# Layer 1 of the last two batches from edge lists for six of eight node tiles

## The chip, the cores and the metric

The kernel runs on one core of a Trainium2 chip. The time is the device time of one execution in microseconds (us), and the figure is the median over several runs. A profiled execution has its own time and a span from its first to its last instruction. In the profile, PE is TensorE, PEld its weight loads, DVE VectorE, ACT ScalarE, POOL GpSimd and SP SyncE, which here only issues DMAs.

## The reference, cut to what matters

Sixteen batches of 1024 nodes with 256 features go through four graph layers. All share one weighted adjacency matrix of 1024 x 1024, in which about 1.6% of the entries (some 17 of a row) are not zero.

```python
x, adj: (16, 1024, 256), (1024, 1024)      # float32
# layer 0: scores only matter where A is not zero
S   = sigmoid(relu(pre_u[:, :, None] + pre_v[:, None] + b1) @ W2 + b2)
a_t = einsum('buv,bud->bvd', S * A, h);  m_t = einsum('uv,bud->bvd', A, h) * h
x   = beta1 * h + beta2 * (a_t @ Wa + ba) + beta3 * (m_t @ Wm + bm)
# layer 1: the layer that is changed
msg = einsum('ij,bjd->bid', A, x)
msg = einsum('bid,ed->bie', msg, W) + b
x   = x + relu(msg)
# layers 2 and 3: attention with a bias
feats = x @ W1.T;  f1 = feats @ W2 + b2
coefs = softmax(leaky_relu(f1[:, :, None] + f1[:, None, :]) + A, axis=-1)
x     = coefs @ feats + bias2 + x
```

## The kernel before

**Groups and pairs.** Batches are taken in four groups of four. For every group, `with_edges` multiplies the scored adjacency with the features (layer 0's edge part), and then `pair_layers` takes the group's batches two by two through layers 1, 2 and 3. The state of a batch is `z`, features on partitions, 2 x 1024 per partition.

**Layer 1 by matmul.** `pair_layers` first projects: `y = z W`, nodes on partitions, 32 matmuls for the two batches, each bank evacuated by ScalarE (L1102). Then, for each half of the nodes, SP loads eight 128x512 blocks of the transposed adjacency from DRAM (`adjT_in`, L1111, three buffers), and TensorE multiplies each with both batches' `y`. ScalarE adds the bias and applies ReLU (L1122), VectorE adds the result to `z` (L1123).

**Layers 2 and 3.** `front` computes features (`feats`, `g_wT`), and `sums` has VectorE build the weights `m` tile by tile (L1033) for TensorE to multiply with `feats`. `finish` scales the result, transposes (L1141, L1165) and adds it.

**Lists.** At the start the kernel finds each node's neighbours: `slot_v` holds up to 32 neighbour numbers of each node and `slot_a` their weights. The first 16 are used directly. Of the rest, in fours, only those groups that are not empty are packed into `XT` = 6 extra tiles of 128 rows (`x_node`, `x_a`); `to_u` says in which row of these each group lies. The lists serve layer 0's scores: GpSimd gathers rows of `v_d` by `slot_v` with an indirect DMA (`fetch`, `gather`, L692), VectorE and ScalarE compute the score (L802, L804, L808), and GpSimd scatters it into `dense_d` (L697).

**Order.** Main work is a generator that yields its estimated TensorE time in us; `Side.along` runs `rate` steps of the side work for each such microsecond. `RATE[1]` is 0.255 beside groups. `paced` makes an instruction wait for the matmul six before the latest one written, so that it does not run ahead of TensorE. Matmuls are recorded by `product` (L125). Instructions on one engine execute in the order of a compile-time schedule, which may differ from the order in which they are written. The side work of a group (its scores) has to be finished before the group's `with_edges`; beside the fourth group there is none left.

```python
for g in range(NGR):
    hw, z = loaded.pop(0)
    while g not in finished:
        next(side.steps)
    side.along(with_edges(g, hw, z), RATE[1])
    side.along(pair_layers(g * GB, z[:2], lambda: None), RATE[1])
    side.along(pair_layers(g * GB + 2, z[2:], lambda: ahead(g + 1)), RATE[1])
```

Of the kernel before, what the change touches and what calls it, by code (L numbers as in the profile page):

```python
# [9 lines left out]
F32 = mybir.dt.float32  # L10
I32 = mybir.dt.int32
U32 = mybir.dt.uint32
AF = mybir.ActivationFunctionType
ALU = mybir.AluOpType
AX = mybir.AxisListType
P = 128

GB = 4
BUFS = 2
RATE = (0.26, 0.255)  # L20
SLOTS = 32
FIRST = 16
EXTRA = SLOTS - FIRST
QUAD = 4
ZERO = 1024
NG = EXTRA // QUAD
XT = 6
HOLD = 40
LEAD = 4
TOP = 16.0  # L30

# [6 lines left out]
def after(tc, ins, others, kind, why):  # L38
    dep = mybir.DependencyInfo(kind, mybir.DependencyReason.DATA)
    for o in others:  # L40
        tc.add_manual_dep(ins.ins, o.ins.name, dep, reason=why)
# [23 lines left out]
def gnn_stack_kernel(  # L65
# [27 lines left out]
    nc = tc.nc  # L93
    B, N, D = x.shape
    NT = N // P
    DH = D // P
    HN = 512
    NV = N // HN
    HT = HN // P
    QN = HN // 2  # L100

    const = ctx.enter_context(tc.tile_pool(name="const", bufs=1))
    dram = ctx.enter_context(tc.tile_pool(name="dram", bufs=1, space=bass.MemoryType.DRAM))
# [3 lines left out]
    def bank():  # L107
        return psum[-1].tile([P, HN], F32, tag="bank", name="bank")
# [8 lines left out]
    def paced(ins, back=6):  # L117


        if recent:  # L120
            after(tc, ins, [recent[max(0, len(recent) - back)]], mybir.DependencyClass.Sync, "keeps pace")
        return ins

    def product(*args, **kw):
        recent.append(nc.tensor.matmul(*args, **kw))  # L125
        del recent[:-BACK]
        return recent[-1]
# [32 lines left out]
    ident = const.tile([P, P], F32, name="ident")  # L160
    make_identity(nc, ident)

    def column(a, name):

        t = const.tile([P, DH], F32, name=name)
        nc.gpsimd.dma_start(t, a.rearrange("(h p) -> p h", p=P))
        return t
# [73 lines left out]
    adjT_d = dram.tile([NT, P, N], F32, name="adjT_d")  # L241
# [3 lines left out]
    NGR = B // GB  # L245
# [9 lines left out]
    TABLE = NG * NT * P  # L255
    WORDS = 16
    extra_d = dram.tile([2 * TABLE, WORDS], F32, name="extra_d")

    slot_v = const.tile([P, NT, SLOTS], U32, name="slot_v")
    slot_a = const.tile([P, NT, SLOTS], F32, name="slot_a")  # L260
# [98 lines left out]
    to_u = const.tile([P, NF], U32, name="to_u")  # L359
    with ExitStack() as stack:  # L360
# [46 lines left out]
        l1b = column(g1_b, "l1b")  # L407
# [44 lines left out]
        ps = bank()  # L452
# [24 lines left out]
        step = 1  # L477
# [10 lines left out]
        to = prep1.tile([P, NF], F32, name="to")  # L488
# [183 lines left out]
    with tc.If(listed > 0) as arm:  # L672
        with ExitStack() as stack:
# [6 lines left out]
            zs = stack.enter_context(tc.tile_pool(name="zs", bufs=2))  # L680
            slot_pool = stack.enter_context(tc.tile_pool(name="slots", bufs=LEAD + 2))
            wide_z = stack.enter_context(tc.tile_pool(name="wide_z", bufs=4))
            wide_t = stack.enter_context(tc.tile_pool(name="wide_t", bufs=5))
            psum_pool(stack, "banks", 8)
            gd_pool = stack.enter_context(tc.tile_pool(name="gd", bufs=4))
# [5 lines left out]
            def gather(dst, src, at, **how):  # L691
                return nc.gpsimd.indirect_dma_start(  # L692
                    out=dst, out_offset=None, in_=src[:], in_offset=bass.IndirectOffsetOnAxis(ap=at, axis=0), **how,
                )
# [6 lines left out]
            def score_steps(pool):  # L701
# [41 lines left out]
                for t in range(NT):  # L743
                    search(own, t)
                    if t == 0:
                        sources(us, *tiles[0])
                        for step in todo[:LEAD]:
                            fetch(us, zt, *step)
# [31 lines left out]
                for n, (g, t, k) in enumerate(todo):  # L780
                    if n + LEAD < len(todo):
                        last = fetch(us, zt, *todo[n + LEAD])
                    for _ in range(0 if n < HOLD else 2 if n % 2 and len(waiting) > 4 else 1):
                        if waiting:
# [53 lines left out]
            def lists(t):  # L838
                if t < NT:
                    return FIRST, slot_v[:, t, :], slot_at[:, t, :], slot_a[:, t, :]  # L840
                return QUAD, x_node[:, t - NT, 1:], x_at[:, t - NT, :], x_a[:, t - NT, :]

            def sources(us, g, t):

                u = us[g, t] = zs.tile([P, GB * D], F32, tag="u", name="u")
                paced(nc.scalar.activation(
                    u.rearrange("p (c k) -> p c k", k=D), b1r[:, None, :].to_broadcast([P, GB, D]), AF.Copy
                ))
                if t < NT:
                    nc.gpsimd.dma_start(u, u_d[g][t * P : (t + 1) * P, :], accum_op=ALU.add)  # L850
                else:
                    gather(u, u_d[g], x_node[:, t - NT, 0:1], compute_op=ALU.add)
# [5 lines left out]
            class Side:  # L858
# [2 lines left out]
                def __init__(self, steps):  # L861
                    self.steps, self.owed = steps, 0.0

                def along(self, main, rate):
                    for us in main:
                        self.owed += us * rate
                        while self.owed >= 1:
                            self.owed -= 1
                            next(self.steps, None)
# [34 lines left out]
            with ExitStack() as first:  # L904
                own1 = first.enter_context(tc.tile_pool(name="own1", bufs=1))
                st_pool = first.enter_context(tc.tile_pool(name="st", bufs=2))
                side = Side(score_steps(own1))
# [49 lines left out]
            three = stack.enter_context(tc.tile_pool(name="three", bufs=3))  # L957
            four = stack.enter_context(tc.tile_pool(name="four", bufs=4))
# [65 lines left out]
            def sums(made, v, finish):  # L1024

                if "f" not in made:
                    catch_up()
                f, r, ta = made["f"], made["r"], made["ta"]
                cols = slice(v * HN, (v + 1) * HN)
                acc = [bank() for _ in range(HT)]  # L1030
                for jt in range(NT):
                    m = four.tile([P, HN], F32, tag="m", name="m")
                    nc.vector.scalar_tensor_tensor(  # L1033
                        m, r[:, cols], ta[:, jt : jt + 1], ea[:, jt, cols], ALU.max, ALU.mult
                    )
                    for c in range(HT):
                        product(
                            acc[c][:, : D + 1], m[:, c * P : (c + 1) * P], f[:, jt, :],
                            start=jt == 0, stop=jt == NT - 1,
                        )  # L1040
                    if jt == 0:
                        catch_up()
                    yield 1.7
                share = small.tile([P, HT], F32, tag="share", name="share")
                for c in range(HT):
                    nc.vector.reciprocal(share[:, c : c + 1], acc[c][:, D : D + 1])
                finish(v, acc, share)
                yield 1.2
# [37 lines left out]
                                ALU.add, ALU.add,  # L1086
                            )

            def pair_layers(b, z, ahead):


                y = [node_major("y") for _ in range(2)]
                for jt in range(0, NT, 2):
                    for i in range(2):
                        ps = bank()
# [7 lines left out]
                            y[i][:, jt : jt + 2, :], ps.rearrange("p (t d) -> p t d", t=2), AF.Copy  # L1103
                        )
                        yield 1.7
                for v in range(NV):
                    cols = slice(v * HN, (v + 1) * HN)
                    acc = [[bank() for _ in range(DH)] for _ in range(2)]
                    for jt in range(NT):
                        a = three.tile([P, HN], F32, tag="a", name="adjT_in")  # L1110
                        nc.sync.dma_start(a, adjT_d[jt][:, cols])  # L1111
                        for i in range(2):
                            for eh in range(DH):
                                product(
                                    acc[i][eh], y[i][:, jt, eh * P : (eh + 1) * P], a,
                                    start=jt == 0, stop=jt == NT - 1,
                                )
                        yield 3.4
                    for i in range(2):
                        for eh in range(DH):  # L1120
                            r = four.tile([P, HN], F32, tag="m", name="r")
                            nc.scalar.activation(r, acc[i][eh], AF.Relu, bias=l1b[:, eh : eh + 1])  # L1122
                            nc.vector.tensor_tensor(z[i][:, eh, cols], z[i][:, eh, cols], r, ALU.add)  # L1123


                def second(i):
# [70 lines left out]
            def ahead(g):  # L1197
                if g < NGR:
                    loaded.append(([load_hw(g * GB + i) for i in range(GB)], load_z(g)))
                    for load, i in z_loads:  # L1200
                        load(i)
                    z_loads.clear()

            for g in range(NGR):
                hw, z = loaded.pop(0)
                while g not in finished:
                    next(side.steps)
                side.along(with_edges(g, hw, z), RATE[1])
                side.along(pair_layers(g * GB, z[:2], lambda: None), RATE[1])
                side.along(pair_layers(g * GB + 2, z[2:], lambda: ahead(g + 1)), RATE[1])  # L1210
            assert next(side.steps, "end") == "end"
            psum.pop()

    with arm.Else():
        with ExitStack() as stack:
# [3 lines left out]
            part = stack.enter_context(tc.tile_pool(name="dpart", bufs=4))  # L1219
# [122 lines left out]
```

## Time and profile before

| | us |
|---|---|
| median of 3 runs | 3267.06 (3267.03 to 3274.82) |
| profiled execution, its own time | 3256.96 |
| its span | 3255.1 |
| TensorE busy | 3157.5 (97%) |
| VectorE busy | 2342.4 (72%) |
| ScalarE busy | 1879.1 (58%) |
| GpSimd busy | 1665.6 (51%) |

The granted clock of TensorE was 0.992 on the mean. Times in the trace are counted from the span's start. A float32 matmul appears as two records. GpSimd's indirect DMAs show as POOL instructions while their descriptors are made; the data arrive later ("landing"). A share of busy time is a mean over very different stages, so the stage around the change has to be read by itself: the fourth group's two pairs, from about 2812 us to the end.

### The profile page before, as it was taken

The page shows a single profiled execution, that of the slowest core. Times are in us where ns is not written, and L with a number is a line of the kernel's source. Part 1 is how long each engine was busy: PE and PEld are TensorE (multiplying, and loading weights), DVE is VectorE, ACT ScalarE, POOL GpSimd, SP SyncE. Part 2 cuts the span into 40 slices and gives each one's busy share as a digit, 9 for nine tenths or more (in the row PEclk, how much of TensorE's full clock was granted, in tenths as well). Part 3 has the DMA queues.
Part 4 walks back from the last instruction along what each step waited for, and adds up shares of the span by engine and source line. Part 5 has one row for each costly group of instructions (what it writes and reads, how often), then busy time and mean ns, then how long its engine had stood idle before and what let it go on. Part 6 is the DMA issues. An engine that isn't in the chain of part 4 may idle for free. (4 is left out here: it accounts for less than half of the span.)

```text
span 3255.1 us, 38756 instructions
## 1 busy us (share of the span) xinstructions
PE 3157.5 (97%) x12162; PEld 2206.3 (68%) x12162; DVE 2342.4 (72%) x3217; ACT 1879.1 (58%) x6316; POOL 1665.6 (51%) x1338
## 2 busy tenths in 40 slices
PE   8899999999997999999999999999999999999999
PEld 5444545545456678578776867778686788778688
DVE  7787767777774799789678979877898881035154
ACT  3245556655667766566886656688666555322132
POOL 1156887686764666657566666665676650000000
PEclk9999999999998999999999999999999999999999
DMA  8998888878798755656875575597656635210100
GB/s 304 327 325 299 281 281 273 273 212 269 242 327 311 219 162 163 203 154 204 292 230 174 154 221 151 183 297 229 180 150 210 186 105 167 84 35 14 55 1 27
DMA packets 268438, 648.91 MB, mean 199 GB/s; under 512 B 42864, under 2 KB 131952, under 8 KB 261056
## 3 DMA queue, kind: packets, MB, share of 16 engines
q0 software_dynamic: 116704, 350.04, 36.8%
q1 hardware_dynamic: 123536, 244.66, 21.8%
q10 hardware_dynamic: 27984, 51.65, 4.2%
q8 instruction: 97, 1.59, 0.2%
q14 instruction: 117, 0.96, 0.1%
HBM read 518.84 MB, written 127.39 MB: 199 GB/s over the span
## 5 line engine op out<-in xcount | busy, mean ns | idle before, releaser
L808 ACT ACTIVATE z<-z 128x256 f32<-128x256 f32 x2432 | 979.7, 406 | 707.3 <-DVE z L804 678.2
L802 DVE TENSOR_TENSOR z<-z,u 128x1024 f32<-128x1024 f32 x608 | 738.8, 1220 | 408.2 <-PE bank L125 276.2
L125 PE MATMUL bank<-feats,m 128*128 128x257 f32 x4096 | 922.1, 383 | 20.8 <-DVE m L1033 18.7
L692 POOL DMA_INDIRECT z<-v_d,slot_v x512 | 645.9, 1262 | 463.8 <-ACT z L808 227.7
L125 PEld LDWEIGHTS bank<-feats,m 128*128 128x128 f32 x4096 | 766.3, 191 | 148.6 <-DVE m L1033 28.6
L804 DVE SCALAR_TENSOR_TENSOR z<-z,w2r 128x1024 f32<-128x1024 f32 x608 | 737.3, 1219 | 8.5
L697 POOL DMA_INDIRECT dense_d<-gt,slot_at x512 | 639.2, 1249 | 197.9 <-issue 134.7
L125 PE MATMUL bank<-gc,hw 128*128 128x256 f32 x2048 | 455.6, 384 | 30.5 <-ACT gc L1061 27.7
L808 ACT ACTIVATION_READ_ACCUMULATOR z<-z 128x1 f32 x2432 | 461.2, 190 | 0.0
L125 PEld LDWEIGHTS bank<-gc,hw 128*128 128x128 f32 x2048 | 387.2, 191 | 98.2 <-ACT gc L1061 40.4
L1033 DVE SCALAR_TENSOR_TENSOR m<-rho,tau,adj_sb 128x512 f32<-128x512 f32 x512 | 374.0, 743 | 107.7 <-PE bank L125 105.1
L125 PE MATMUL bank<-adj_sb,h 128*128 128x512 f32 x1024 | 442.4, 592 | 2.2 <-ACT st L318 2.1
L125 PE MATMUL bank<-adjT_in,y 128*128 128x512 f32 x1024 | 441.3, 592 | 1.4 <-DMA adjT_in<-adjT_d 1.4
L125 PEld LDWEIGHTS bank<-adjT_in,y 128*128 128x128 f32 x1024 | 194.4, 190 | 243.6 <-issue 228.6
L125 PEld LDWEIGHTS bank<-adj_sb,h 128*128 128x128 f32 x1024 | 194.4, 190 | 242.2 <-issue 237.7
L125 PE MATMUL bank<-w,hT 128*128 128x512 f32 (+1 forms) x1024 | 335.8, 488 | 6.8 <-DMA w<-in_L_gnn_W_dram 6.5
L1061 ACT ACTIVATE gc<-gd 128x1024 f32<-128x1024 f32 x128 | 265.5, 2074 | 88.2 <-PE bank L125 60.0
L125 PEld LDWEIGHTS bank<-w,hT 128*128 128x128 f32 x1024 | 195.0, 191 | 150.6 <-issue 126.3
L125 PE MATMUL bank<-g_wT,z 128*128 128x257 f32 x1024 | 232.9, 382 | 0.2 <-ACT st L1171 0.2
L692 POOL DMA_INDIRECT z<-v_d,x_node x96 | 127.1, 1324 | 181.8 <-ACT z L808 118.0
L125 PEld LDWEIGHTS bank<-g_wT,z 128*128 128x128 f32 x1024 | 192.9, 191 | 30.9 <-issue 3.8
L1123 DVE TENSOR_TENSOR z<-z,r 128x512 f32<-128x512 f32 x64 | 42.5, 689 | 135.2 <-ACT r L1122 134.9
(150 smaller groups left out, 2183.4 us busy)
## 6 DMA issues: line engine op xcount, KB each, us to landing
gd<-dense_d SPq DMA_DIRECT2D x128, 512.0 KB, 5.0
dense_d<-zero ACTq DMA_DIRECT2D x64, 512.0 KB, 5.9
adjT_in<-adjT_d SPq DMA_DIRECT2D x128, 256.0 KB, 3.3
h<-in_x_dram SPq DMA_DIRECT2D x19, 1024.0 KB, 12.9
u_d<-st SPq DMA_DIRECT2D x64, 256.0 KB, 5.7
v_d<-st SPq DMA_DIRECT2D x64, 256.0 KB, 6.5
hw_d<-st SPq DMA_DIRECT2D x64, 256.0 KB, 6.5
u<-u_d POOLq DMA_DIRECT2D x32, 512.0 KB, 8.1
```

Of the source, the lines that this page charges most:

```text
L125: recent.append(nc.tensor.matmul(*args, **kw))
L692: return nc.gpsimd.indirect_dma_start(out=dst, out_offset=None, in_=src[:], in_offset=bass.IndirectOffsetOnAxis(ap=at, axis=0), **how,)
L697: return nc.gpsimd.indirect_dma_start(out=dst[:], out_offset=bass.IndirectOffsetOnAxis(ap=at, axis=0), in_=src, in_offset=None,)
L802: paced(nc.vector.tensor_tensor(z, z, u, ALU.add))
L804: nc.vector.scalar_tensor_tensor(zk, zk, 0.0, w2r[:, None, :].to_broadcast([P, GB, D]), ALU.max, ALU.mult)
L808: nc.scalar.activation(zk[:, c, :], zk[:, c, :], AF.Copy, accum_out=s[:, k, c : c + 1])
L1033: nc.vector.scalar_tensor_tensor(m, r[:, cols], ta[:, jt : jt + 1], ea[:, jt, cols], ALU.max, ALU.mult)
L1061: paced(nc.scalar.activation(gc, gd.rearrange("p n i -> p i n"), AF.Copy), 16)
L1123: nc.vector.tensor_tensor(z[i][:, eh, cols], z[i][:, eh, cols], r, ALU.add)
```

## The change

Only the fourth group is treated differently. Its second pair's projection `y` is computed right after `with_edges`, before the first pair (`far_ahead`), and stored to DRAM as `y_d`, one row of 512 numbers (both batches) per node. For node tiles 6 and 7 (`FAR` = 6) the neighbour product stays a matmul with 256 columns of the adjacency. For node tiles 0 to 5, `by_lists` sums it along the first pair's work, 144 steps of one gather and one VectorE instruction:

- 24 steps for the extra tiles, four rows each, into `part`; each finished tile is stored by SP to `part_d`,
- 96 steps for the first 16 neighbours of the nodes of tiles 0 to 5, into `msg`,
- 24 steps that fetch the extra rows' sums from `part_d` and add them to `msg`.

Four gathers are issued ahead of the step that uses them, and `slot_pool` has six buffers. The rate is 0.75 steps per main microsecond for the first 68 (layer 1 of the first pair), then 0.55; what remains then is written in one piece after the first pair. At the head of the second pair `from_lists` transposes `msg` on TensorE, four tiles and then two, and applies bias, ReLU and the add as before (`onto`).

```diff
+FAR = 6
+    y_d = dram.tile([N, 2 * D], F32, name="y_d")
+    part_d = dram.tile([XT * P + P, 2 * D], F32, name="part_d")
...
+            def neighbours(y, z, cols):
+                n = cols.stop - cols.start
+                acc = [[bank() for _ in range(DH)] for _ in range(2)]
+                for jt in range(NT):
+                    a = three.tile([P, HN], F32, tag="a", name="adjT_in")[:, :n]
+                    nc.sync.dma_start(a, adjT_d[jt][:, cols])
+                    for i in range(2):
+                        for eh in range(DH):
+                            product(
+                                acc[i][eh][:, :n], y[i][:, jt, eh * P : (eh + 1) * P], a,
+                                start=jt == 0, stop=jt == NT - 1,
+                            )
+                    yield 3.4 * n / HN
+                onto(z, cols, lambda i, eh: acc[i][eh][:, :n])
...
+            def by_lists(msg):
+                spares = [gd_pool.tile([P, QN, GB], F32, tag="gd", name="msg") for _ in range(4)]
...
+                msg.extend(halves[:FAR])
+                part = halves[FAR:]
+                nc.gpsimd.memset(part[0], 0.0)
+                nc.sync.dma_start(part_d[XT * P :, :], part[0])
+                nc.vector.tensor_scalar(to_u, to_u, float(XT * P), None, ALU.min)
+                todo = [(NT + i, k) for i in range(XT) for k in range(QUAD)]
+                todo += [(t, k) for t in range(FAR) for k in range(FIRST)]
+                todo += [(t, FIRST + q) for t in range(FAR) for q in range(NG)]
...
+                for n, (t, k) in enumerate(todo):
+                    if n + LEAD < len(todo):
+                        fetch_row(*todo[n + LEAD])
+                    z = got.pop((t, k))
+                    to = msg[t] if t < NT else part[t % len(part)]
+                    if t < NT and k >= FIRST:
+                        paced(nc.vector.tensor_tensor(to, to, z, ALU.add))
+                    elif k == 0:
+                        paced(nc.vector.tensor_scalar(to, z, lists(t)[3][:, k : k + 1], None, ALU.mult))
+                    else:
+                        paced(nc.vector.scalar_tensor_tensor(
+                            to, z, lists(t)[3][:, k : k + 1], to, ALU.mult, ALU.add
+                        ))
+                    if t >= NT and k == QUAD - 1:
+                        nc.sync.dma_start(part_d[(t - NT) * P : (t - NT + 1) * P, :], to)
+                    yield
+            def from_lists(z, msg):
+                for t0 in range(0, FAR, HT):
...
+                                nc.tensor.transpose(ps[:, c * P : (c + 1) * P], msg[t][:, at : at + P], ident)
+                    yield 1.2
+                    n = len(tiles) * P
+                    onto(z, slice(t0 * P, t0 * P + n), lambda i, eh: turned_back[i, eh][:, :n])
...
+            def far_ahead(z, main):
+                y = yield from projected(z)
+                both = y_d.rearrange("(t p) (i d) -> p t i d", p=P, i=2)
+                for i in range(2):
+                    nc.sync.dma_start(both[:, :, i, :], y[i])
+                yield from neighbours(y, z, slice(FAR * P, N))
+                gone, far = 0.0, Side(by_lists(msg))
+                def slots():
+                    nonlocal gone
+                    for us in main:
+                        gone += us
+                        yield us * (0.75 if gone < 68 else 0.55)
+                far.along(slots())
+                for _ in far.steps:
+                    pass
+                yield 0
...
-                side.along(pair_layers(g * GB, z[:2], lambda: None), RATE[1])
-                side.along(pair_layers(g * GB + 2, z[2:], lambda: ahead(g + 1)), RATE[1])
+                one = pair_layers(g * GB, z[:2], lambda: None, layer_one(z[:2]))
+                if g < NGR - 1:
+                    side.along(one, RATE[1])
+                    side.along(pair_layers(g * GB + 2, z[2:], lambda: ahead(g + 1), layer_one(z[2:])), RATE[1])
+                else:
+                    for _ in far_ahead(z[2:], one):
+                        pass
+                    for _ in pair_layers(g * GB + 2, z[2:], lambda: None, from_lists(z[2:], msg)):
+                        pass
```

`projected`, `neighbours`, `onto` and `layer_one` hold what stood at the head of `pair_layers`; `layer_one` does what it did there.

## The prediction

> **What bounds the kernel now.** The page first: engine shares, then the slices.
>
> ```profile
> PE 3157.5 (97%) x12162; PEld 2206.3 (68%) x12162; DVE 2342.4 (72%) x3217; ACT 1879.1 (58%) x6316; POOL 1665.6 (51%) x1338
> ...
> DVE  7787767777774799789678979877898881035154
> POOL 1156887686764666657566666665676650000000
> ...
> DMA  8998888878798755656875575597656635210100
> ```
>
> TensorE is busy for 97% of the span. The last seven slices, some 570 us, have no GpSimd work, little DMA and a half idle VectorE: this is the last group, whose edge scores are finished. The chain of waits for that stretch is TensorE alone:
>
> ```profile
> 2701.78 187.94 PE bank L125 x744
> ...
> 3030.79 77.44 PE bank L125 x232
> 3108.23 0.87 PE bank L999 x8
> ```
>
> So a microsecond of matmul removed there is a microsecond gained, if nothing else makes TensorE wait. TensorE's timeline gives layer 1 of the two pairs:
>
> ```profile
> 2812.13 13.98 PE L125 MATMUL bank<-l1wT,z 128*128 128x256 f32 x64
> 2825.94 55.10 PE L125 MATMUL bank<-adjT_in,y 128*128 128x512 f32 x128
> ...
> 3030.63 13.98 PE L125 MATMUL bank<-l1wT,z 128*128 128x256 f32 x64
> 3044.45 55.10 PE L125 MATMUL bank<-adjT_in,y 128*128 128x512 f32 x128
> 3099.38 8.85 PE L125 MATMUL bank<-g_wT,z 128*128 128x257 f32 x40
> ```
>
> A matmul is two records, so the neighbour product is 64 matmuls in 55.1 us. A pair lasts from 2812.1 to 3030.6, 218.5 us: 69 of layer 1 (phase 1) and 149 of attention (phase 2). What side work does to a pair is read from windows over the third group's first pair (2252 on) and the last group's first (2812 on); columns are the window, its length, busy TensorE, weight loads, VectorE, ScalarE, GpSimd, then clock, DMA share, GB/s.
>
> ```profile
> 2252.00:2321.00 69.00, 69.00 (x195) 36.71 (x194) 48.69 (x51) 40.01 (x162) 48.31 (x40) 1.00 0.73 213
> 2330.00:2478.00 148.00, 143.41 (x698) 121.82 (x696) 146.97 (x231) 102.00 (x382) 106.41 (x78) 1.00 0.55 154
> 2883.00:3031.00 148.00, 148.00 (x733) 130.24 (x733) 75.52 (x154) 41.95 (x96) 0.00 (x0) 1.00 0.04 12
> ```
>
> With scores beside it phase 1 loses nothing; phase 2, VectorE full (147 of 148), loses some 7 us (2329.4 to 2477.9 against 2889.6 to 3030.6). The gathers' durations in those two phases, phase 1 first (minimum, median, maximum in ns):
>
> ```profile
> L692 POOL DMA_INDIRECT z<-v_d,slot_v x16: 938/982/1937, 2251.2 to 2310.4; - x16
> L692 POOL DMA_INDIRECT z<-v_d,slot_v x30: 959/1498/2663, 2331.4 to 2476.4; - x30
> ```
>
> Back-to-back GpSimd DMAs start 0.30 us after one another ends, so one costs 1.28 us undisturbed and 1.8 beside a full VectorE.
>
> **What the Trainium skill says.** "GPSIMD Engine Reference", 1. Specifications: GpSimd's SBUF interfaces are shared with VectorE, with contention from VectorE instructions with two SBUF inputs. The trace agrees: 982 ns against 1498, and the list sums are such instructions. "DMA: Bandwidth & Descriptors", Queues, rings and completion order: SP has one ring on each engine, consumed in order. The trace agrees: a 512 KB `gd` load issued 0.4 us after a 1 MB `z` load landed after 7.0 us, against 3.4 alone. "TensorE: Matmul & The Clock Gate", What's actually happening: after an idle window of about 3.4 us the clock is halved until TensorE is busy again. The trace agrees: after 15.5 us idle, at 994, the clock was 0.60 for 6 us, some 2.4 us lost.
>
> **The change, part by part** (all in the last group).
>
> *Removed.* Six of eight column tiles of the last pair's neighbour product: 55.1 x 6/8 = 41.3 us. The rest is 32 matmuls of 256 columns at 0.434 (257 columns: 64 records in 13.88), 13.9 instead of 13.8. Added: 24 transposes at 0.109 (8 in 0.87), 2.6 us. **Net on TensorE: -38.6 us.** The moved projection (13.9 us) costs the same where it now stands. ScalarE's and VectorE's bias, ReLU and add keep their element count: nothing.
>
> *Storing `y`.* Two 1 MB stores on SP's queue, the second when the last `y` tile is evacuated, 0.7 us after the projection. Then come SP's loads of adjT for the quarter product. Those with free buffers (three) can be issued earlier: engines here do not keep program order (at 3015.29 an `m` L1033 runs ahead of `st` L1175, written before it). Three loads cover 3 x 1.74 = 5.2 us. The fourth lies behind 2 MB: at 290 GB/s (from the 1.5 MB above in 7.4 us, 2 off for latency) it lands 9.4 us after the projection. TensorE waits about **4 us**; none if the stores move in the shadow, 9 to 11 if no load is ahead. The gathers wait for both stores too; they have landed about 10 us after the projection, while the product runs, so the first six (all that `slot_pool` holds) are ready when the first pair begins.
>
> *List steps in phase 1.* There are 24 + 96 + 24 = 144 steps: one gather of 128 rows of 2 KB and one VectorE instruction of 128x512, priced by `m` at 0.75 us. Phase 1 takes 68 x 0.75 = 51. VectorE: 51 x 0.75 = 38 of 69 us, against 48.7 in the third group at no loss. GpSimd: 45 gathers after the head start, at 1.5, 68 us: just enough. New here is SP: six stores of partial sums wait for VectorE steps, which are paced behind TensorE, and the first pair's adjT loads queue behind them. A load is needed every 3.45 us and lands in 3.3; a store late by more than the buffers' slack holds TensorE. **3 us**, from 0 (six times hidden) to 8 (over 1 us each).
>
> *List steps in phase 2.* 146 x 0.55 = 80. VectorE: 75.5 + 80 x 0.75 = 135 of 148 us (91%), in order, with `m` behind steps that may wait for a gather. The full VectorE cost 7; I take **4**, from 1 to 10. GpSimd has 80 gathers, and the last ones: at 1.65, between the two phases' costs, 132 us. Landing takes 5 to 8; six slots give 10.
>
> *The remainder.* 131 steps are done by the pair's end, 13 are left, and they may run only when TensorE is six matmuls from that end. Data for six are there; seven gathers follow, a slot freed for each: first at 1.9 us before the end, the seventh at -1.9 + 6 x 1.6 = 7.7, landing 4.5 later, step 0.7, transposes 0.9: 13.8 us after the end. Otherwise TensorE would go on after 0.9 + 2.6 = 3.5. In between it can do 3.5 us of the features of node tiles 0 to 3, if they are issued first. So 6.8 to 10.3 us, and up to 2.4 for the clock: **9.5**, from 4 (features of both batches fill it) to 16.
>
> *Sum.* -38.6 + 4 + 3 + 4 + 9.5 = -18. The profiled execution took 3256.96 us (span 3255.1, 1.9 around it), 10 less than the median of 3267.06; the difference carries over: 3249.
>
> **The rivals.**
> *Nearly all is gained.* Loads ahead of the stores, partial sums early, transposes delayed behind features: 30 to 37 us, 3230 to 3237. For it: phase 1 of the third group lost nothing with more VectorE work. Against: the 13 steps are written after all of the pair's matmuls.
> *The stalls add up.* Each cost in its upper half (8 + 6 + 7 + 13 = 34): -5, so 3262, between 3257 and 3276.
> *GpSimd becomes the bound: slower.* From phase 2's start 93 gathers remain. The group's path from the end of the edge product to the last pair's attention is 218.5 + 69 = 287.5 us now. Bound by gathers it is 13.9 + 4 + 13.9 + 69 + 93r + 7.5: equal at r = 1.93 us. r = 2.1 gives +16, 3283. For it: the median of 1.8 beside a full VectorE, and five at 1.93 + 0.3 = 2.2. Against: steps are 0.75 us long where scores were 1.22, and VectorE has gaps. Should the schedule keep the gathers from starting before the pair ends, so that the lists do not run along it, 144 x 1.28 = 184 us would stand bare, less 38.6; nothing suggests that.
>
> **How the numbers follow.** Forecast (11 to 30 gained) 0.48; nearly all 0.14; adding up 0.24; GpSimd-bound 0.14. Within 0.3% (10 us, about what a measurement of this kernel can tell from no change: its runs span 7.8) is the third case. So faster 0.62, same 0.24, slower 0.14. The likeliest case alone is 3237 to 3256. The range for 8 in 10 reaches from the best case's lower part, 3230, into the slower case, to 3279.
>
> **What would show it.** Right: 24 transposes and half the `adjT_in` records in the last pair; one idle stretch of TensorE of some 4 us after the first projection and one of 7 to 12 before the last pair's features, released by a DMA or a list step; VectorE near 90% in phase 2; gathers at 1.3 to 1.4 us mean there. Wrong: gathers of 1.6 and more with VectorE waiting on them throughout, phase 1 stretched by adjT loads, or no idle TensorE at the joint.

## The result, and the profile after

The change is faster, by about as much as forecast: 3251.42 us (3244.91 to 3264.24, nine runs) against 3270.32 (3260.66 to 3279.44, nine runs of the kernel before, taken with it). The ratio is 0.9945, with a 95% interval from 0.9926 to 0.9963, so 12 to 24 us. A later set on another occasion gave 3229.51 against 3251.66, ratio 0.9931 (0.9917 to 0.9944).

The spans of the two profiled executions hide this: 3255.1 before, 3255.8 after. TensorE's timeline of the kernel after says why (start, length, engine, line, operation, out<-in, records, and in brackets the idle time before it).

```profile
2686.24 15.97 PE L126 MATMUL bank<-feats,m 128*128 128x257 f32 x60 [4.63 <-issue]
...
2717.68 110.67 PE L126 MATMUL bank<-gc,hw 128*128 128x256 f32 x512
2828.19 13.98 PE L126 MATMUL bank<-l1wT,z 128*128 128x256 f32 x64
2842.00 5.34 PE L126 MATMUL bank<-adjT_in,y 128*128 128x256 f32 x24
2847.18 2.32 PE L126 MATMUL bank<-l1wT,z 128*128 128x256 f32 x10
...
2870.58 13.90 PE L126 MATMUL bank<-adjT_in,y 128*128 128x512 f32 x32
2886.17 34.57 PE L126 MATMUL bank<-adjT_in,y 128*128 128x512 f32 x80 [1.69 <-DMA adjT_in<-adjT_d]
2922.56 7.13 PE L126 MATMUL bank<-adjT_in,y 128*128 128x512 f32 x16 [1.82 <-issue]
...
2947.76 3.65 PE L126 MATMUL bank<-feats,m 128*128 128x257 f32 x8 [3.08 <-DVE m L1038]
...
3249.28 1.04 PE L1243 MATMUL bank<-ident,z 128*128 128x128 f32 x8
```

The same two ends in the kernel before:

```profile
2701.62 110.67 PE L125 MATMUL bank<-gc,hw 128*128 128x256 f32 x512
...
3248.26 1.04 PE L1165 MATMUL bank<-ident,z 128*128 128x128 f32 x8
```

The last group's edge product (`gc,hw`) starts at 2717.7 here and at 2701.6 in the execution before. Those 16 us arose in earlier groups, where the source is the same; one 4.6 us idle piece is the first line above. (Over the twelve profiles of this document the start lies between 2693.6 and 2722.2.) The edit must therefore be read inside the group: from the start of the edge product to the start of the last eight transposes it took 2701.6 to 3248.3 before, **546.6 us**, and 2717.7 to 3249.3 after, **531.6 us**.

The page of the kernel after shows where the added work went.

```profile
PE 3132.2 (96%) x12122; PEld 2203.5 (68%) x12122; DVE 2433.7 (75%) x3366; ACT 1880.1 (58%) x6320; POOL 1826.6 (56%) x1483
...
DVE  7787777777775799799668979867898872148754
POOL 1146888676664666657566666665676550066600
```

VectorE has 91 us more, GpSimd 161, and both fill slices 36 to 38 (counted from 1), where GpSimd had nothing. The price of the joint between the two pairs stands in the same timeline, a few lines on:

```profile
3084.38 1.47 PE L1193 MATMUL bank<-ident,msg 128*128 128x128 f32 x12
3089.36 0.66 PE L1193 MATMUL bank<-ident,msg 128*128 128x128 f32 x4 [3.51 <-DVE msg L1172]
3095.50 1.09 PE L1193 MATMUL bank<-ident,msg 128*128 128x128 f32 x4 [5.48 <-issue]
3096.38 6.09 PE L126 MATMUL bank<-g_wT,z 128*128 128x257 f32 x16
3102.31 0.60 PE L1193 MATMUL bank<-ident,msg 128*128 128x128 f32 x4
3103.77 5.48 PE L126 MATMUL bank<-g_wT,z 128*128 128x257 f32 x24 [0.86 <-DVE z L1117]
3109.09 1.04 PE L1004 MATMUL bank<-ident,feats 128*128 128x128 f32 x8
```

The joint is measured from the first transpose of `msg` to the features' own transposes (L1004): 24.7 us. Features alone took 8.7 before (3099.4 to 3108.1) and the 24 transposes need 2.6, so 13.4 us are lost. TensorE idles 9.9 us in three pieces, and the 16 records after it take 6.1 us instead of the 3.5 of their usual 0.217 each: the granted clock over them was 0.59.

### The profile page after: what moved, and what is told of

Read it like the earlier page. It is cut to its first block, busy times and chain, and to the rows that moved or that the text cites. A ratio compares the mean times of both kernels' runs of the same rounds, so it can differ in the third digit from the quotient of the medians.

```text
span 3255.8 us, 39220 instructions
## 1 busy us (share of the span) xinstructions
PE 3132.2 (96%) x12122; PEld 2203.5 (68%) x12122; DVE 2433.7 (75%) x3366; ACT 1880.1 (58%) x6320; POOL 1826.6 (56%) x1483
## 5 line engine op out<-in xcount | busy, mean ns | idle before, releaser
L697 POOL DMA_INDIRECT z<-v_d,slot_v x512 | 655.1, 1279 | 471.2 <-ACT z L813 241.6
L126 PE MATMUL bank<-adjT_in,y 128*128 128x512 f32 (+1 forms) x960 | 401.5, 579 | 5.1 <-DMA adjT_in<-adjT_d 2.6
L126 PEld LDWEIGHTS bank<-adjT_in,y 128*128 128x128 f32 x960 | 181.8, 190 | 220.4 <-issue 207.6
L697 POOL DMA_INDIRECT z<-y_d,slot_v x96 | 107.4, 1119 | 62.5 <-DVE msg L1176 41.7
```

The lines of the kernel that those rows point to most:

```text
L697: return nc.gpsimd.indirect_dma_start(out=dst, out_offset=None, in_=src[:], in_offset=bass.IndirectOffsetOnAxis(ap=at, axis=0), **how,)
```

## The experiments

All times below are read off TensorE's timeline of each kernel. Phase 1 counts only the first pair's neighbour product (55 us if nothing waits), phase 2 goes from there to the first transpose of `msg` (149.76 if nothing waits), joint is as above. "Group" is the whole stretch of 546.6 before (546.5 in expectations below). Each row is one profiled execution; e3, e4 and e7 were executed only that once (3252.87, 3255.96 and 3226.57 us), so from them nothing but the trace is read.

| kernel | phase 1 | phase 2 | joint | group |
|---|---|---|---|---|
| change (first profile) | 59.0 | 154.9 | 24.7 | 531.6 |
| e1 no list steps | 54.9 | 149.8 | 11.8 | 509.1 |
| e2 rate 0.65 | 56.9 | 156.1 | 11.8 | 517.8 |
| e3 stores on ScalarE | 54.9 | 157.6 | 24.1 | 529.2 |
| e4 gathers only | 62.5 | 151.8 | 17.1 | 523.9 |
| e5 rate 0.65 and stores | 55.1 | 149.8 | 11.8 | 509.9 |
| e6 five tiles | 55.7 | 149.8 | 11.8 | 516.3 |
| e7 sums only | 54.9 | 149.8 | 19.4 | 516.6 |
| e8 ten gathers ahead | 55.7 | 149.8 | 18.8 | 516.8 |
| e9 the change again | 56.6 | 149.8 | 25.0 | 524.5 |
| e10 as e5, again | 54.9 | 149.8 | 11.8 | 509.0 |

**e1: no list steps.** How much is there to gain at all?

```diff
                 todo += [(t, FIRST + q) for t in range(FAR) for q in range(NG)]
+                for m in msg:
+                    nc.vector.memset(m, 0.0)
+                todo = []
```

> Left out: all 144 list steps (no gather, no sum); the sums are set to zero, so layer 1 of the last two batches lacks six node tiles' neighbours. Everything else of the change stays: y stored, quarter product, 24 transposes. Theory (the matmuls taken out are worth 38.6 us and the list work gives back some 23 of it: 4 in phase 1, 5 in phase 2, 13 at the joint): last group 546.5 - 38.6 = 508 to 510 us in the trace, median some 36 us below the kernel before. Rival (the gain is limited by storing y or by something before the lists): the last group stays at 520 us or more.

Measured: group 509.1, 37.5 us under the kernel before; median 3235.3 against 3270.12, ratio 0.9893 (0.9865 to 0.9922). So the matmuls taken out are worth what was summed, less 1 us lost around the stored `y` and at the joint, and the list work gives back all the rest: 22.5 us in that first profile.

**e2: nothing left at the joint.**

```diff
-                        yield us * (0.75 if gone < 68 else 0.55)
+                        yield us * (0.75 if gone < 68 else 0.65)
```

> Only the second rate changes, 0.55 to 0.65, so that 146 x 0.65 = 95 steps run in phase 2 and none are left at the joint. Theory (13 us are lost at the joint because 12 steps are left there and their gathers come one by one): idle TensorE at the joint falls from some 13 to 3 us, phase 2 grows by 1 to 3, and the last group takes 521 to 525 us against 531.6. Rival (GpSimd's gathers are the bound all along, so the work only moves): phase 2 grows by about 10 us and the group stays within 3 us of 531.6.

Measured: the joint falls from 24.7 to 11.8, exactly that of e1; phase 2 grows by 1.2. The group takes 517.8, less than expected, because next to nothing was lost at the joint where 3 us had been put and phase 1 lost 2 us less. Median 3237.34 against 3270.12, ratio 0.9902 (0.9884 to 0.9920). TensorE's timeline at the joint:

```profile
3069.84 2.78 PE L1193 MATMUL bank<-ident,msg 128*128 128x128 f32 x24
3072.87 8.95 PE L126 MATMUL bank<-g_wT,z 128*128 128x257 f32 x40 [0.25 <-DVE z L1117]
```

All 24 transposes go in one piece and the features follow after 0.25 us. The loss at the joint is the steps left over, and GpSimd and VectorE had room for them earlier.

**e3: the stores of partial sums on another queue.**

```diff
-                        nc.sync.dma_start(part_d[(t - NT) * P : (t - NT + 1) * P, :], to)
+                        nc.scalar.dma_start(part_d[(t - NT) * P : (t - NT + 1) * P, :], to)
```

> The six stores of partial sums are issued by ScalarE instead of SyncE. Theory (they hold up the adjacency loads behind them on SyncE's queue): the two or three pauses in the first pair's neighbour product, 3.9 us in sum (58.95 us against 55.1), shrink to under 1.5. Rival (the loads are late because gathers and stores fill the DMA engines): the pauses stay at 3 to 4 us.

Measured: the neighbour product takes 54.9 us, with no pause. SyncE's queue in the kernel after (`SPq`: DMAs that SyncE issues) shows what had happened:

```profile
2843.93 15.52 SPq L1124 DMA_DIRECT2D adjT_in<-adjT_d  x8
2862.62 10.27 SPq L1180 DMA_DIRECT2D part_d<-msg  x3
2874.21 0.32 SPq L1124 DMA_DIRECT2D adjT_in<-adjT_d  x1
2879.90 0.32 SPq L1180 DMA_DIRECT2D part_d<-msg  x1
2880.32 2.04 SPq L1124 DMA_DIRECT2D adjT_in<-adjT_d  x2
...
2893.46 0.32 SPq L1180 DMA_DIRECT2D part_d<-msg  x1
...
2907.04 3.75 SPq L1124 DMA_DIRECT2D adjT_in<-adjT_d  x2
...
2918.48 0.32 SPq L1124 DMA_DIRECT2D adjT_in<-adjT_d  x1
```

The store issued at 2879.90 waited for its VectorE step; the adjacency load behind it went out at 2880.32, and TensorE, which needed it at 2884.5, got it at 2886.2. That is 5.9 us after its issue, against a median of 3.3 in the kernel before, so busy DMA engines may have used up the slack. The theory stands for this first pause. In e7, where the stores stay on SyncE's queue but no step waits for a gather and no gather fills the DMA engines, the same load went out 7.4 us into the product instead of 9.7, and the product took 54.9 us. The second pause of the kernel after, 1.8 us at 2922.6, is not explained by stores. The last of them went out at 2893.46, yet SyncE issued the load of 2918.48 eight us after the one before it (2910.5), where 3.4 is usual. Why is not known, and that e3 has no such pause does not show that the stores caused it. In the later profiles phase 1 takes 55.7 to 56.6 us with the stores on SyncE's queue (e6, e8, e9) and 54.9 to 55.1 with them on ScalarE's (e5, e10), so there the stores cost 0.7 to 1.6 us. Phase 2 of e3 lost 7.8 us; see e5 for that.

**e4: gathers without sums, and e7: sums without gathers.** In e4 the loop keeps `fetch_row`, each gather `paced` itself, and leaves out the VectorE instruction and the stores; `msg` is zero, and zeros are stored to `part_d` once, ahead of the loop. In e7 six rows are fetched and the steps read those:

```diff
-                    if n + LEAD < len(todo):
-                        fetch_row(*todo[n + LEAD])
-                    z = got.pop((t, k))
+                    z = zs6[n % len(zs6)]
```

> Left out: the 144 VectorE sums (msg is zero); the 144 gathers stay, each paced behind TensorE itself; partial sums are zeros stored once. Theory (phase 2's 5 us are VectorE's, in order before m): phase 2 back at 149.8 to 151 us, joint 6 to 9 us, shorter since VectorE steps no longer alternate; a gather's median in phase 2 falls from 1.21 us towards 0.95, since VectorE's two-input instructions are fewer. Rival (gathers themselves disturb TensorE or VectorE through SBUF or DMA): phase 2 stays at 153 us or more.

> Left out: all gathers but the first six; the 144 VectorE steps read those six buffers again and again, so the sums are wrong data. Theory (VectorE's steps alone cost TensorE little; a pause near the start of phase 2 and the joint's gathers are what is lost): phase 2 at 150 to 152 us, joint (from the first transpose of msg to the features' own transposes) 17 to 19 us against 24.7 with gathers and 11.9 without lists. Rival (VectorE in order before m is what costs phase 2): 153 us or more.

Measured in e4: phase 2 took 151.8, of which 1.8 is one piece of idle TensorE. The gathers by their durations in phase 2 (minimum, median, maximum in ns), the kernel after first, then e4:

```profile
L697 POOL DMA_INDIRECT z<-y_d,slot_v x68: 943/1212/1474, 2928.7 to 3053.1; - x68
```

```profile
L697 POOL DMA_INDIRECT z<-y_d,slot_v x67: 940/944/1408, 2937.1 to 3061.0; - x67
```

Without the sums the median falls from 1212 to 944 ns. With VectorE's two-input steps beside them, the making of descriptors took 28% longer, which agrees with the Trainium skill, "GPSIMD Engine Reference", 1. Specifications: GpSimd shares its SBUF interfaces with VectorE, and instructions with two SBUF inputs contend for them. Two results don't fit the expectation. The neighbour product paused 5.2 us for an adjacency load, which SyncE issued late though no store of partial sums stood on its queue. And the joint took 17.1 although its transposes went in one piece, because ScalarE evacuated a feature tile 3.3 us late and the clock dropped. The trace doesn't say why SyncE and ScalarE were late.

Measured in e7: phase 2 at 149.76, no loss at all with the same VectorE work, so the rival falls. The joint of 19.4 is 7.6 above e1's: that is VectorE's share of the remainder.

**e5 and e10: both edits.** The diffs of e2 and e3 together.

> Rate 0.65 in phase 2 and the stores of partial sums on ScalarE's queue, together. Theory (joint and stores are separate losses): the group falls from 517.8 us (rate alone) by the 2 us that its first pair's neighbour product still loses, to 515 to 517; median 30 to 36 us under the kernel before. Rival (the stores held GpSimd's and VectorE's steps back in a useful way, so that the steps now crowd the start of phase 2): phase 2 grows by as much as phase 1 shrinks, group 517 to 520.

Measured: 3214.11 against 3254.60, ratio 0.9881 (0.9864 to 0.9897). The group took 509.9, below the 515 to 517 expected: phase 2 took 149.8, less than e2 and e3 had. The windows of the same kernel's second profile (e10) show phase 1, phase 2 and joint; columns as in the windows of before:

```profile
2859.00:2914.00 55.00, 55.00 (x131) 24.54 (x130) 33.15 (x47) 5.17 (x8) 42.50 (x42) 1.00 0.86 282
2914.00:3064.00 150.00, 150.00 (x742) 131.80 (x741) 132.30 (x251) 44.02 (x98) 103.78 (x90) 1.00 0.64 170
3064.00:3076.00 12.00, 11.75 (x68) 10.36 (x66) 7.02 (x16) 5.33 (x13) 0.00 (x0) 1.00 0.14 45
```

TensorE is busy in all of the first two windows, VectorE 88% of phase 2. What phase 2 lost in the first set was thus not the list steps by themselves.

**e6: five tiles instead of six.** `FAR = 5`, with two of the spare halves for `part`; it leaves no remainder at the old rates.

> Five node tiles from lists instead of six, rates as in the change: 124 steps, so none are left at the joint. It gives back 55.1/8 = 6.9 us of matmul, less 4 transposes. Theory (the remainder at the joint costs 13 us): group 531.6 + 6.5 - 12.5 = 525 to 527 us, faster than with six tiles although TensorE does more. Rival (the joint is slow for its chain of transposes, ReLU and adds and not for the steps left): 536 us or more.

Measured: group 516.3, 8.2 us less than the change's second profile, although TensorE multiplies 6.9 us more. That is also below the 525 to 527 expected, which had been counted from the first profile with its pauses. Median 3220.61, ratio 0.9898 (0.9881 to 0.9914). A second way to the same conclusion: the remainder, not the chain of transpose, ReLU and add, makes the joint slow.

**e8: gathers further ahead.** Each slot buffer is used as two halves, and `LEAD` in the list loop becomes 10.

> Twelve half buffers in place of six, ten gathers ahead of their step in place of four; rates as in the change. Theory (at the joint eight gathers go out one by one, 1.3 us each, and land 6 us later): most of the 12 left steps find their data there, so the joint falls from 24.7 to 18 to 20 us, VectorE's 12 x 0.7 us still standing. Rival (GpSimd is at its limit in phase 2 and cannot run ahead): joint 23 us or more. The pauses in phases 1 and 2 are expected unchanged within 2 us.

Measured: joint 18.8, as expected; phase 2 at 149.8 and phase 1 at 55.7, where the first profile's pauses had been expected again; 3223.44, ratio 0.9903 (0.9886 to 0.9920). VectorE at the joint, now with all data there:

```profile
3060.66 1.27 DVE L1258 TENSOR_TENSOR st<-st,bank 128x512 f32<-128x512 f32 x2
3061.85 5.50 DVE L1177 TENSOR_TENSOR msg<-msg,z 128x512 f32<-128x512 f32 x9
3067.27 0.68 DVE L1117 TENSOR_TENSOR z<-z,r 128x512 f32<-128x512 f32 x1
```

Nine steps run in one piece. In the change, the same stretch shows steps waiting for gathers (GpSimd and VectorE of the kernel after):

```profile
3090.43 0.94 POOL L697 DMA_INDIRECT z<-part_d,to_u  x1 [0.30 <-issue]
3091.37 0.69 DVE L1172 TENSOR_TENSOR msg<-msg,z 128x512 f32<-128x512 f32 x1 [2.06 <-DMA z<-part_d,to_u]
3091.68 1.20 POOL L697 DMA_INDIRECT z<-part_d,to_u  x1 [0.30 <-issue]
3093.07 0.69 DVE L1172 TENSOR_TENSOR msg<-msg,z 128x512 f32<-128x512 f32 x1 [1.01 <-DMA z<-part_d,to_u]
3093.19 1.40 POOL L697 DMA_INDIRECT z<-part_d,to_u  x1 [0.30 <-issue]
```

So of the joint's 13 us over e1, some 6 are gathers that are late (25.0 to 18.8) and 7 are VectorE's steps and TensorE's restart (18.8 to 11.8).

**e9: the change again**, beside e10.

> The changed kernel itself once more, beside the two-edit version. In the first set of runs, phase 2 lost 2 to 8 us in every kernel with gathers, in pauses of 3 to 5 us in which ScalarE or VectorE started late and no wait in the trace explains it; in the second set it took exactly 149.76 us in all four kernels. Theory (those pauses belong to the execution and not to the list steps): phase 2 at 149.8 to 151 us unless such a pause is seen again, phase 1 at 56 to 59 and the joint at 23 to 25 us as before. Rival (VectorE's steps cost phase 2 some 5 us with rate 0.55 in this kernel): 153 us or more without a pause.

> The version with rate 0.65 and partial sums stored from ScalarE's queue, on the same chip as the changed kernel. Theory: group at 509 to 512 us and 13 to 20 us faster than the changed kernel in the median, of which joint 12.8 and stores 2 to 4. Rival (its lead in the second set was the chip's): within 8 us of the changed kernel.

Measured: the change at 3229.51, the version with both edits at 3215.87, against 3251.66; ratios 0.9931 (0.9917 to 0.9944) and 0.9887 (0.9872 to 0.9902). In the traces 524.5 and 509.0. The change's phase 2 is at 149.8, its joint unchanged:

```profile
3052.85 1.47 PE L1193 MATMUL bank<-ident,msg 128*128 128x128 f32 x12
3057.56 1.12 PE L1193 MATMUL bank<-ident,msg 128*128 128x128 f32 x4 [3.24 <-DVE msg L1172]
3064.18 1.08 PE L1193 MATMUL bank<-ident,msg 128*128 128x128 f32 x4 [5.50 <-DVE msg L1172]
```

The theory stands: phase 2's 5 us in the first profile belong to that execution. Joint and stores remain: 13.2 + 1.6 of the 15.5 between the two traces; the other 0.7 lie ahead of phase 1.

## Why the prediction was right

The forecast of 3249 (-18) met 3251.42 (-18.9), and it was the likeliest case that came. Its core is shown: the matmuls taken out are gained in full, and stalls give back about half. The terms of these stalls, though, were not all right. Two misses cancelled, and pauses of the first profile filled in for a third, so the close number is in part luck.

| step | forecast | first profile | e9 |
|---|---|---|---|
| matmuls less transposes | -38.6 | -38.6 | -38.6 |
| store ahead of the loads | +4 | +0.9 | +0.9 |
| phase 1, stores on SyncE's queue | +3 | +4.0 (1.8 of it another pause) | +1.6 |
| phase 2, VectorE in order | +4 | +5.1 | 0 |
| joint | +9.5 | +13.4 | +13.7 |
| sum | -18 | -15.2 | -22.4 |
| group, from the traces | | -15.0 | -22.2 |

- **The matmuls** were right; e1 shows 37.5 with 1 us of other losses in it.
- **The store ahead of the loads** was too dear. Three loads did go ahead of it and did cover 5.2 us (24 records from 2842.0), as assumed. But TensorE then took up the next pair's projection (10 records at 2847.2) instead of waiting; the idle stretch of some 4 us that was named as a sign did not come (0.35). The step assumed TensorE to be in written order, which the same paragraph had just denied for other engines. `y` landed 7.3 us after the projection, not 10.
- **Phase 1** had the right mechanism, shown by SyncE's queue and by e5, e7 and e10 as well as e3, but was put too high: 0.7 to 2.0 us in e2, e6, e8 and e9. The 4.0 of the first profile hold the second pause, 1.8 us, which no store explains.
- **Phase 2** was an error hidden by an accident. Steps were costed from a full VectorE (147 of 148 us); the steps took 128 of 155, and e5 to e10 show no loss up to 88%. The 5 us of the first profile agree with the 4 forecast only because of pauses that the same code did not show again in e9.
- **The joint** was mis-sized, term by term. Forecast were seven gathers from 1.9 us before the pair's end, the last at 7.7 after it; eight started after the end, the last at 9.7 (3083.5 to 3093.2). The step of the last gather was to begin 4.5 us after the gather's start; it began 7.3 after (3093.2 to 3100.5). The restart of the clock, put at up to 2.4, cost 2.6, and the ReLU and add before the features were left out of the chain. Features of tiles 0 to 3 did run ahead of the last tile's transposes, but behind the fifth's.
- **GpSimd as the bound** did not come: a gather costs 1.13 us on the mean in phase 2, 1.43 with the 0.30 gap, against the 1.93 at which the gain would have gone. **The stalls add up** did not come, nor did **nearly all is gained**; but the latter was in reach, and e5 and e10 reach it (509.9 and 509.0, where e1 has 509.1).

## What to carry to other kernels

When side work is spread along main work by a rate, count its steps against the length of its cover: twelve of 144 left over cost as much as a third of what the edit saved, while the covering stage had room for them at no cost. A store that waits for one engine's late steps is better kept off the queue that feeds another: here it cost 0.7 to 2.0 us, and nothing in e7, where the steps waited for no gather. And when two executions differ by 16 us ahead of the edit, compare the edited stretch between the same two instructions, not the spans.

## What was not expected of the hardware

- **A VectorE 88% busy did not slow TensorE.** At 132.3 of 150 us, in order with the weights `m`, phase 2 took its undisturbed 149.76 us. In the kernel before, at 99% and beside the scores of the third group, it had lost 7; where between the two the loss begins was not measured.
- **Pauses without a cause in the trace.** The change's first profile and e2, e3 and e4 lost 2 to 8 us near the start of phase 2, where ScalarE or VectorE started late though the trace shows nothing that held them (in e3 ScalarE stood for 6.8 us). The second pause in the change's phase 1 and the 5.2 us of e4 look the same, with SyncE late. e1, without gathers, has none, nor has any of the later six profiles, though e9 runs the same code as the first. Neither the list steps nor the gathers alone explain them; what they are stays open.
- **Idle TensorE costs twice.** After 9.9 us of idle pieces, 16 records took 6.1 us instead of 3.5. This agrees with the Trainium skill, "TensorE: Matmul & The Clock Gate", What's actually happening: the clock is halved after an idle window of about 3.4 us and returns only after about as long a busy one. No single piece needed to be that long: in e7, after 2.1 and 2.4 us of idle time with 0.66 us of transposes between them, the granted clock was 0.50 from 3064.5 to 3068.3.
